# Column halves in an attention's closing step and a new state space model, in a four-layer graph network on one Trainium2 core

## The chip, the core and the metric

The kernel runs on one core of a Trainium2 chip. Its metric is the device time of one execution in microseconds (us). The kernel before takes 2626.57 us, the median of three runs that lie between 2625.1 and 2631.52 us.

The engines appear in the profile as PE (TensorE, matrix multiplication), PEld (its weight loads), DVE (VectorE), ACT (ScalarE), POOL (GpSimd) and SP (SyncE). [...]

## What is computed

The input is a matrix `x` of 2708 nodes by 256 features and a 0/1 adjacency matrix. Four layers follow one another, each a graph layer and a feed-forward layer, with a normalisation ahead of each and an addition to `x` behind it:

- layer 0: cosine attention over the graph, then the slice layer
- layer 1: graph attention with four heads, then a top-1 choice of eight experts
- layer 2: graph attention with biases, then a decoder layer (attention with a triangular mask, then the top two of eight experts)
- layer 3: graph attention with elu, then a linear layer

Two of the feed-forward layers are touched. The slice layer, with 8 heads of 64 features and 64 slices per head, is

```python
sw = softmax((xm @ W_slice.T + b_slice) / temp, axis=-1)      # [head, node, slice]
st = einsum('bhnc,bhng->bhgc', fx, sw) / (sw.sum(2) + 1e-05)  # slice tokens: 64 x 512
ot = _hydra(st, ...)                                         # state space model over 64 tokens
out = einsum('bhgc,bhng->bhnc', ot, sw); out @ out_w.T + out_b
```

and its state space model, which runs over the 64 tokens `u` in both directions, is

```python
z, xBC, dt = split(u @ in_w.T)                 # 512, 640 (x 512, B 64, C 64), 2 x 8 columns
dt = softplus(dt + dt_bias)                    # one set of 8 for each direction
xBC = silu(causal convolution of xBC, 3 taps, + conv_b)
h = h * exp(-dt * exp(A_log)) + dt * B * x     # per head and token; y = h . C
y = shift(y_forward) + shift(y_backward) + x * (x @ fcD_w.T + Dp)
yg = y * silu(z)
yg = yg * rsqrt(mean(yg**2) + 1e-05) * norm_w
return yg @ out_w.T
```

The decoder's attention has four query heads and two heads of keys and values, of 64 features each. Its output goes through `wo`, is added to the normalised input, and is routed to the experts.

## The kernel before

All activations stay on the chip in `X`, 22 tiles of 128 nodes (the last has 20). Buffers come from pools. The program's scheduler settles the order in which each engine issues its instructions, by data, buffers and priorities, except where a block fixes the order of an engine to that of the code (`manual_schedule`).

**Slice layer (`slice_ffn`, L392 to L478).** First it issues the loads of weights on POOL's queue: `outw`, `outb`, `wfx`, `bfx`, `hyin` (2336 KB) and `hyout` (1024 KB). Then `ln_stats` takes mean and variance of every tile on DVE. The loop over tiles is a pipeline of three steps: `logits` (normalise on DVE, transpose and multiply on PE), `softmax` (five operations of 128x512 and a small reciprocal on DVE, an exponential on ACT) and `products` (four transposes `pt` and four matmuls into the accumulators `z` on PE). After the last tile, L468 divides the four accumulators by their norms and gives `zs`, the slice tokens weighted with the features.

**State space model (`hydra`, L481 to L672).** It runs alone between the tile loop and the output: `zs` is transposed (L504), multiplied by `wfx` for each head (L512), copied to `u`, transposed again to `ut`. From `ut` come the gate `z` (eight matmuls of 512 columns in all), `dt`, and the convolution inputs (L539). The recurrence is unrolled: the sums of decays between each pair of tokens are made by matmuls of the 64x64 triangular matrices with the decays (L615 to L619), an exponential turns them into kernels `k`, one for each direction, and the two kernels are merged into `km` (64 x 8 x 64) on DVE. Then `py = km x` on PE (L650), the gate, the norm on DVE and ACT, another transposition `yt`, the output product with `hyout` (32 matmul instructions, each with 64 columns), and eight products with `outw` that are copied into `mix`. The constants (`dtb`, `alog`, conv taps, triangular masks, `fcd`, `dp`, `normw`) are loaded or made inside this function. Its PSUM pool has three buffers. Every engine's order is the scheduler's. After it, a loop over 22 tiles multiplies `swt` by `mix` and adds to `X` (L478).

**Decoder attention (L1860 to L2135).** The nodes are cut into column chunks `cols` of 512 queries, numbered n = 0 to 4, and a last one, 5, of 148. Each chunk has two pairs of heads (p = 0, 1); the last chunk takes both pairs together. PE's order is written by hand; the others are the scheduler's. Five kinds of work are woven together, as generators that are advanced one step at a time:

- `scores(n, p, j)` and `values(n, p, j)`: scores of key tile j against the queries of chunk n (L1974), exponential on ACT, sums on DVE (L2005), and values on PE (L1999). They go in groups of two; the values of a group follow the scores of the next.
- `close(n, p)` (L2007 to L2016): when the last key tile is through, matmuls with ones give the sums of exponentials `pd`, DVE takes the reciprocal (L2015) and multiplies by the accumulated output `po` (L2016), which gives `yt`.
- `send(n)`: `yt` times `wo` (`wy`, L139), addition to the normalised input (`xa`, L2031), addition into `X` on POOL (L2032), router logits, choice and ranking of experts (`rank`, L1630), and the rows scattered to memory in expert order by indirect DMAs on POOL (`hs`, L1651). The generator `sends` (L2088) starts `send(n)` as soon as both pairs of chunk n are closed, and advances it one step in each group.
- `project(n)`: transposes, values, and the rotated keys and queries of chunk n (`tp`, `pv`, `pj` with L1945 and L1948). The generator `projects` runs it one chunk ahead; each group advances it so far as the share of the chunk's groups that are through demands, and to its end before the chunk's first scores.

The auxiliary PSUM buffers (`aux`, two of them) are shared by `pd`, `wy`, `tp`, `pv`, `pj` and the router.

Of the kernel before, what the change touches and what calls it, by code (L numbers as in the profile page):

```python
# [392 lines left out]
def slice_ffn(net, wf, bf, early):  # L393
# [3 lines left out]
    with ExitStack() as ctx:  # L397
# [5 lines left out]
        with ExitStack() as c2:  # L403
            wp = c2.enter_context(tc.tile_pool(name="s_w", bufs=1))
            zs = wp.tile([P, 4, D + 1], F32, name="zs")
            wfx = net.load_weight(wp, a["w_fxT"], "wfx")
            bfx = wp.tile([1, HC], F32, name="bfx")
            nc.gpsimd.dma_start(bfx, a["b_fx"].partition_broadcast(1))
            hyin = net.load_weight(wp, a["hy_inT"], "hyin")
            hyout = net.load_weight(wp, a["hy_outT"], "hyout")  # L410
# [60 lines left out]
            hydra(net, wp, zs, wfx, bfx, hyin, hyout, outw, mix)  # L471
# [9 lines left out]
def hydra(net, wp, zs, wfx, bfx, hyin, hyout, outw, mix):  # L481


    nc, tc, a = net.nc, net.tc, net.a
    H, L, HC = 8, 64, 512
    ident = net.ident
    with tc.tile_pool(name="h_w", bufs=1) as w, tc.tile_pool(name="h_p", bufs=3, space=PSUM) as psum:

        def transposes(src, n, name):

            ps = psum.tile([P, n, L], F32, name="hp", tag="hp")
            for m in range(n):
                nc.tensor.transpose(ps[:, m, :], src[:, m * P : (m + 1) * P], ident[:L, :L])
            t = w.tile([P, n, L], F32, name=name)
            nc.scalar.copy(t, ps)
            return t


        zt = w.tile([P, 2, HC], F32, name="zt")
        ztr = w.tile([1, HC], F32, name="ztr")  # L500
        for c in range(2):
            ps = psum.tile([P, HC], F32, name="hp", tag="hp")
            for m in range(4):
                nc.tensor.transpose(ps[:, m * P : (m + 1) * P], zs[:, m, c * P : (c + 1) * P], ident)  # L504
            nc.scalar.copy(zt[:, c, :], ps)
        ps = psum.tile([1, HC], F32, name="hp", tag="hp")
        for m in range(4):
            nc.tensor.transpose(ps[:, m * P : (m + 1) * P], zs[:, m, D : D + 1], ident)
        nc.scalar.copy(ztr, ps)
        ps = psum.tile([L, HC], F32, name="hp", tag="hp")  # L510
        for h in range(H):
            hs = slice(h * L, (h + 1) * L)  # L512
            net.matmul_k(ps[:, hs], zt[:, :, hs], wfx[:, :, hs], last=False)
            nc.tensor.matmul(ps[:, hs], ztr[:, hs], bfx[:, hs], start=False, stop=True)
        u = w.tile([L, HC], F32, name="u")
        nc.scalar.copy(u, ps)
        ut = transposes(u, 4, "ut")


        pz = psum.tile([L, HC], F32, name="hp", tag="hp")  # L520
        net.matmul_k(pz, ut, hyin[:, :, 0:HC])
        zg = w.tile([L, HC], F32, name="zg")
        nc.scalar.activation(zg, pz, AF.Silu)
        pdt = psum.tile([L, 2, H], F32, name="hp", tag="hp")
        net.matmul_k(pdt.rearrange("p a h -> p (a h)"), ut, hyin[:, :, 1152:1168])
        dt = w.tile([L, 2, H], F32, name="dt")
        dtb = net.load_rows(w, a["dt_bias"], H, "dtb", L)
        nc.vector.tensor_tensor(dt, pdt, dtb.unsqueeze(1).to_broadcast([L, 2, H]), ALU.add)

        def conv(n, parts, offset, name):  # L530

            cw = w.tile([parts, n, 3], F32, name=f"cw{name}")
            nc.gpsimd.dma_start(
                cw, a["conv_w"][offset : offset + n * parts].rearrange("(n p) k -> p n k", p=parts)
            )
            cb = w.tile([parts, n], F32, name=f"cb{name}")
            nc.gpsimd.dma_start(cb, a["conv_b"][offset : offset + n * parts].rearrange("(n p) -> p n", p=parts))
            ps = psum.tile([parts, n, L], F32, name="hp", tag="hp")
            for m in range(n):  # L539
                o = HC + offset + m * parts  # L540
                net.matmul_k(ps[:, m, :], hyin[:, :, o : o + parts], ut)
            pad = w.tile([parts, n, L + 2], F32, name=f"pad{name}")
            nc.vector.memset(pad, 0.0)
            nc.scalar.copy(pad[:, :, 2:], ps)
            y = w.tile([parts, n, L], F32, name=f"y{name}")
            for m in range(n):
                nc.vector.tensor_scalar(
                    y[:, m, :], pad[:, m, 0:L], cw[:, m, 0:1], cb[:, m : m + 1], ALU.mult, ALU.add
                )
                for k in (1, 2):  # L550
                    nc.vector.scalar_tensor_tensor(
                        y[:, m, :], pad[:, m, k : k + L], cw[:, m, k : k + 1], y[:, m, :], ALU.mult, ALU.add
                    )
            nc.scalar.activation(y, y, AF.Silu)
            return y

        xt = conv(4, P, 0, "x")
        bc = conv(2, L, HC, "bc")
        ps = psum.tile([L, HC], F32, name="hp", tag="hp")
        for m in range(4):  # L560
            nc.tensor.transpose(ps[:, m * P : (m + 1) * P], xt[:, m, :], ident)
# [1285 lines left out]
def attention(net, route, ln2, router, weights, mixture):  # L1847
# [11 lines left out]
    with ExitStack() as ctx:  # L1859
# [228 lines left out]
        def sends():  # L2088
            for n in range(len(cols) - 1):
                while n not in closed:  # L2090
                    yield
# [419 lines left out]
```

## Time and profile before

One execution was profiled. It took 2629.6 us itself; the span of its instructions is 2627.7 us.

| | before |
|---|---|
| median of three runs | 2626.57 us |
| profiled execution, time and span | 2629.6 us, 2627.7 us |
| mean granted clock of TensorE | 0.962 |
| busy PE, DVE, ACT, POOL | 2440.1, 1479.9, 1057.7, 335.0 us |
| slice layer, load issues to first `pt` on PE | 388.08 to 410.54 us |
| state space model, last `zs` to first output matmul | 505.43 to 565.24 us |
| attention | 1535 to 1926 us |

Positions are in us from the start of the span. A line such as `PE wy L139 <- DVE yt L2016: 11.6, 4, 3.4` says that PE stood before work of tile `wy`, line 139, until DVE's work of line 2016 on tile `yt` had ended: 11.6 us in all, four times, 3.4 us the longest. In a line in order of time the columns are start, duration, engine, line, operation, output and inputs, and in square brackets how long the engine stood before it and what ended that. "x6" is a group of six like instructions. PE's clock is granted by a throttle: 1.00 is full speed, 0.50 half. Busy time of PE can include time at half clock.

### The profile page before, as it was taken

The numbers are of one execution on the slowest core, as the hardware profiler recorded it, in microseconds if no ns is written. First come the engines' busy times: TensorE is split into PE (matmuls) and PEld (weight loads), VectorE is DVE, ScalarE is ACT, GpSimd is POOL, SyncE is SP. The second block draws the span as 40 slices with busy tenths as digits, with TensorE's granted clock in tenths as the row PEclk, the third lists the DMA queues.
The fourth block names the chain that finished last, engine by engine and source line by source line (L and its number), as shares of the span: only waits on it lengthen the run. The fifth ranks groups of instructions, "written<-read, shape, count | busy, mean of one in ns | idle before, by whom it ended". The sixth has DMA issues, their size and how long they took to land. (4 is left out here: it accounts for less than half of the span.)

```text
span 2627.7 us, 32580 instructions
## 1 busy us (share of the span) xinstructions
PE 2440.1 (93%) x11674; PEld 1583.9 (60%) x11674; DVE 1479.9 (56%) x3272; ACT 1057.7 (40%) x1703; POOL 335.0 (13%) x471
## 2 busy tenths in 40 slices
PE   5899999979999998979799989999899999969998
PEld 4666765665333334568588854444367777747887
DVE  7754438546888875333554457776752222264556
ACT  3444443224887762311444423334322222234454
POOL 1000002200000000144130011221231111110002
PEclk9999999879999999989899999999989999989999
DMA  8799511000000003664310010000231111050001
GB/s 289 279 295 319 188 66 52 3 6 1 1 1 1 1 3 106 168 192 129 103 48 1 1 39 9 23 15 15 102 133 47 33 33 33 22 204 7 0 1 43
DMA packets 106874, 197.70 MB, mean 75 GB/s; under 512 B 8846, under 2 KB 63736, under 8 KB 103876
## 3 DMA queue, kind: packets, MB, share of 16 engines
q1 hardware_dynamic: 88010, 146.82, 17.8%
q0 software_dynamic: 14896, 43.89, 5.2%
q10 hardware_dynamic: 3806, 4.85, 0.6%
q8 instruction: 98, 1.61, 0.3%
q14 instruction: 64, 0.52, 0.1%
HBM read 135.82 MB, written 59.71 MB: 74 GB/s over the span
## 5 line engine op out<-in xcount | busy, mean ns | idle before, releaser
L701 DVE SCALAR_TENSOR_TENSOR e<-e,mask 128x768 f32<-128x768 f32 (+3 forms) x352 | 417.5, 1217 | 241.2 <-ACT e L700 239.2
L700 ACT ACTIVATE e<-big_p,minus_one,ratio 128x768 f32<-128x768 f32 (+3 forms) x352 | 418.6, 1226 | 280.5 <-PE acc L1432 193.1
L1432 PE MATMUL acc<-V,e 128*128 128x257 f32 x1848 | 401.9, 380 | 5.7 <-DVE e L701 5.6
L1432 PEld LDWEIGHTS acc<-V,e 128*128 128x128 f32 x1848 | 350.9, 190 | 56.9 <-issue 7.0
L2186 PE MATMUL h<-w,ft 128*128 (+1 forms) x752 | 234.6, 454 | 1.0 <-DMA f<-hs 1.0
L307 PE MATMUL acc<-F,e 128*128 128x257 f32 (+1 forms) x924 | 212.6, 383 | 4.0 <-DVE e L303 3.6
L897 PE MATMUL acc<-e,V 128*64 128x512 f32 (+1 forms) x1056 | 208.1, 547 | 1.3 <-DVE e L701 1.3
L307 PEld LDWEIGHTS acc<-F,e 128*128 128x128 f32 (+1 forms) x924 | 171.9, 190 | 56.6 <-DVE e L303 29.5
L2203 DVE TENSOR_TENSOR hh<-hh,h 128x682 f32<-128x682 f32 x47 | 40.7, 866 | 243.7 <-PE h L2186 243.7
L2186 PEld LDWEIGHTS h<-w,ft 128*128 128x128 f32 x752 | 136.1, 191 | 56.7 <-issue 1.8
L897 PEld LDWEIGHTS acc<-e,V 128*64 128x64 f32 x1056 | 73.5, 137 | 150.4 <-issue 145.0
L1983 ACT ACTIVATE e<-sc 128x1024 f32<-128x1024 f32 (+4 forms) x131 | 107.1, 863 | 136.7 <-PE sc L1974 116.6
L303 DVE TENSOR_TENSOR e<-e,mask 128x512 f32<-128x512 f32 (+2 forms) x132 | 80.4, 621 | 141.2 <-ACT e L296 139.5
L2005 DVE TENSOR_TENSOR sum<-sum,e 128x1024 f32<-128x1024 f32 (+4 forms) x131 | 134.8, 1029 | 38.3 <-ACT e L1983 23.7
L296 ACT ACTIVATE e<-score 128x512 f32<-128x512 f32 (+2 forms) x132 | 69.4, 544 | 170.8 <-PE score L294 145.4
L2218 PE MATMUL po<-w,ht 114*128 (+1 forms) x564 | 129.8, 380 | 0.9 <-DVE ht L2211 0.9
L1974 PE MATMUL sc<-qt,kt 64*128 64x512 f32 (+5 forms) x568 | 123.9, 555 | 0.9 <-ACT sum L1983 0.9
L2218 PEld LDWEIGHTS po<-w,ht 114*128 114x128 f32 x564 | 106.6, 190 | 22.4 <-DVE ht L2211 8.1
L908 PE MATMUL den<-e,low 128*3 128x512 f32 (+1 forms) x1056 | 117.7, 542 | 0.0
L294 PE MATMUL score<-QK 128*128 128x512 f32 (+2 forms) x264 | 112.2, 554 | 3.4 <-ACT e L296 3.0
L1999 PE MATMUL po<-e,V 128*64 128x512 f32 (+5 forms) x524 | 111.2, 543 | 0.3 <-DVE e L1989 0.3
L2212 ACT COPY ht<-pt 114x256 f32<-114x256 f32 x47 | 17.5, 372 | 200.7 <-DVE ht L2211 200.7
(654 smaller groups left out, 3420.2 us busy)
## 6 DMA issues: line engine op xcount, KB each, us to landing
row<-in_adj SPq DMA_DIRECT2D x21, 1354.0 KB
raw<-in_adjT SPq DMA_DIRECT2D x35, 768.0 KB
hs<-zero SPq DMA_DIRECT2D x8, 2838.0 KB
hidden<-hr SPq DMA_DIRECT2D x32, 256.0 KB
wd<-in_f_wd SPq DMA_DIRECT2D x8, 1024.0 KB
kept<-mask SPq DMA_DIRECT2D x21, 338.5 KB
mask<-kept SPq DMA_DIRECT2D x21, 338.5 KB
w<-in_d_w1T SPq DMA_DIRECT2D x8, 682.0 KB
```

The costliest lines, as they stand in the source:

```text
L294: nc.tensor.matmul(ps[:r, :iw], QK[:, 0, span(j)], QK[:, 1, i0 : i0 + iw], start=True, stop=True)
L307: ended = nc.tensor.matmul(acc[k], e[:r, k * P : (k + 1) * P], F[:r, j, :], start=j == 0, stop=j == NT - 1)
L700: nc.scalar.activation(v, big_p[:, i], AF.Relu, bias=net.minus_one, scale=ratio)
L701: return nc.vector.scalar_tensor_tensor(v, v, 1.0, net.mask[:, j, i], ALU.add, ALU.mult)
L897: nc.tensor.matmul(acc[n][half, :iw], V[:, j, h, :], e[n][:, k, :iw], start=j == 0, stop=j == NT - 1)
L908: nc.tensor.matmul(den[g : g + Q, :iw], low[:, j, h, Q - 1 - q : 2 * Q - 1 - q], e[n][:, k, :iw], start=False, stop=j == NT - 1 and q == Q ...
L1432: nc.tensor.matmul(acc[k][:ri], e[:, k * P : k * P + ri], V[:, j, :], start=j == 0, stop=j == NT - 1)
L1974: nc.tensor.matmul(by_pairs(ps[:r, g], m, iw)[:, :, o:], kt[b, span(j)], qt[b, :, o:iw], start=True, stop=True)
L1999: nc.tensor.matmul(by_pairs(outs[n, p][b], m, iw)[:, :, o:], V[:r, j, g, :], by_pairs(e[:r, g], m, iw)[:, :, o:], start=j == 0, stop=j == ...
L2005: nc.vector.tensor_tensor(total, total, by_heads(e[:r], m, iw)[:, :, :, o:], ALU.add)
L2186: last = nc.tensor.matmul(halves[s, n][:, q, :HALF], fts[s][:, c, :], weights.w13[n][:, es[s], c, q * HALF : (q + 1) * HALF], start=c == 0 ...
L2218: last = nc.tensor.matmul(po, ht[:KP, k, :], w2[:KP, es[s], k, :], start=k == 0, stop=k == KC - 1)
```

## The change

It has three parts. The line numbers of the profile are those of the kernel before.

1. **The closing step.** For the ten closes with one head pair, reciprocal and product are each issued for columns 0 to 255 and for 256 to 511. The last close is left whole.
2. **PE's order in the attention.** `sends` lets two more steps pass between the second close of a chunk and the start of `send`. A counter `quiet` is set to 2 at each close, and while it is positive no step of `projects` is taken, except in the first chunk and where a chunk's projection has to be finished for its scores.
3. **The state space model.** The function `hydra` becomes a class. Its constructor is called where the loads stood, ahead of `ln_stats`. It loads and prepares all constants there: `hyout` is multiplied by `norm_w` row by row (four DVE operations of 128x512), `exp(A_log)` is taken on ACT, triangular masks and zeroed buffers are made on POOL. `run` has a hand-written order on PE, ACT and DVE and seven PSUM buffers. The two directions lie in the two halves of the partitions, so that one DVE or ACT instruction does both; the heads write `ut` directly in transposed form, and everything behind it (gate, `y`, output) stays transposed, so that `u` and `y` are no longer transposed on PE. The gate's product comes late and has 64 columns instead of 512. The norm's sum of squares is a matmul with ones, and its factor is applied at the last eviction, four instructions of 128x256 in turn on ACT and DVE.

The diff, cut to its core:

```diff
-            wfx = net.load_weight(wp, a["w_fxT"], "wfx")
...
-            hyout = net.load_weight(wp, a["hy_outT"], "hyout")
+            layer = Hydra(net, wp)
             ln = net.ln_stats()
...
-            hydra(net, wp, zs, wfx, bfx, hyin, hyout, outw, mix)
+            layer.run(zs, outw, mix)
...
+class Hydra:
+    def __init__(self, net, pool):
...
+        self.wfx = net.load_weight(pool, a["w_fxT"], "wfx")
+        self.bfx = pool.tile([1, HC], F32, name="bfx")
+        nc.gpsimd.dma_start(self.bfx, a["b_fx"].partition_broadcast(1))
+        self.hyin = net.load_weight(pool, a["hy_inT"], "hyin")
+        self.hyout = net.load_weight(pool, a["hy_outT"], "hyout")
+        self.fcd = net.load_weight(pool, a["fcdT"], "fcd")
+        self.dtb = net.load_rows(pool, a["dt_bias"], H, "dtb")
+        self.alog = net.load_rows(pool, a["a_log"], H, "alog")
+        nc.scalar.activation(self.alog, self.alog, AF.Exp)
+        self.dp = pool.tile([H, 1], F32, name="dp")
+        nc.gpsimd.dma_start(self.dp, a["hy_d"].rearrange("(p n) -> p n", n=1))
+        normw = pool.tile([P, 4], F32, name="normw")
+        nc.gpsimd.dma_start(normw, a["norm_w"].rearrange("(c p) -> p c", p=P))
+        for c in range(4):
+            nc.vector.tensor_scalar(self.hyout[:, c, :], self.hyout[:, c, :], normw[:, c : c + 1], None, ALU.mult)
+        for name, n, parts, offset in (("bc", 2, L, HC), ("x", 4, P, 0)):
...
+            nc.gpsimd.memset(pad, 0.0)
...
+        make_upper_triangular(nc, self.seen[low])
+        make_lower_triangular(nc, self.seen[high])
+        make_upper_triangular(nc, self.rise[low])
+        make_upper_triangular(nc, self.rise[high], val=-1.0, diag=False)
+        nc.vector.tensor_scalar(self.fall, self.rise, -1.0, None, ALU.mult)
+        self.pick = pool.tile([H, H, L], F32, name="pick")
+        nc.vector.tensor_copy(self.pick, net.ident[:H, :H].unsqueeze(2).to_broadcast([H, H, L]))
+        self.km = pool.tile([P, H, L], F32, name="km")
+        nc.gpsimd.memset(self.km, 0.0)
+    def run(self, zs, outw, mix):
...
+            ps = bank([P, 4, L])
+            for h in range(H):
+                here = ps[halves[h % 2], h // 2, :]
+                nc.tensor.matmul(here, self.bfx[:, hs], ztr[:, hs], start=True, stop=False, skip_group_check=True)
+                for c in range(2):
+                    nc.tensor.matmul(
+                        here, self.wfx[:, c, hs], zt[:, c, hs], start=False, stop=c == 1, skip_group_check=True
+                    )
...
+            for b in halves:
+                nc.tensor.matmul(
+                    pk[b], self.fall[b], la[b].unsqueeze(2).to_broadcast([L, H, L]),
+                    start=True, stop=False, skip_group_check=True,
+                )
+            for h in range(H):
+                for b in halves:
+                    nc.tensor.matmul(
+                        pk[b, h, :], la[b, h : h + 1].to_broadcast([L, L]), self.rise[b],
+                        start=False, stop=True, skip_group_check=True,
+                    )
...
+            pz = bank([P, 4, L])
+            for m in range(4):
+                net.matmul_k(pz[:, m, :], hyin[:, :, m * P : (m + 1) * P], ut)
...
+            for m in range(4):
+                net.matmul_k(po[:, m, :], self.hyout[:, :, m * P : (m + 1) * P], y)
...
+            for m in range(4):
+                pm = bank([P, D])
+                for b in halves:
+                    nc.tensor.matmul(pm[b], ot[b, m, :], outw[b, m, :], start=True, stop=True, skip_group_check=True)
+                if m % 2:
+                    nc.scalar.activation(mix[:, m, :], pm, AF.Copy, scale=rs)
                 else:
+                    nc.vector.tensor_scalar(mix[:, m, :], pm, rs, None, ALU.mult)
...
-            y = results[n][:, p : p + m, :iw]
-            nc.vector.reciprocal(y, by_pairs(pd, m, iw))
-            nc.vector.tensor_tensor(y, y, by_pairs(outs.pop((n, p)), m, iw), ALU.mult)
+            po = outs.pop((n, p))
+            half = 2 * P if m == 1 else iw
+            for i in range(0, iw, half):
+                y = results[n][:, p : p + m, i : i + half]
+                nc.vector.reciprocal(y, by_pairs(pd, m, iw)[:, :, i : i + half])
+                nc.vector.tensor_tensor(y, y, by_pairs(po, m, iw)[:, :, i : i + half], ALU.mult)
...
                 while n not in closed:
                     yield
+                for _ in range(2):
+                    yield
                 yield from send(n, rp, aux)
...
+                quiet -= 1
                 for n, p in ending:
                     close(n, p)
+                    quiet = 2
...
                 while group and at[2] * len(queries[at[0]]) * (tiles_of(*cols[at[0]])[-1] + 1) < at[1] * 18:
+                    if quiet > 0 and at[0]:
+                        break
                     at[2] += 1
                     next(heads, None)
```

## The prediction

> **What bounds the kernel now.** I read the page's busy shares and clock row first, then the waits of TensorE inside the attention stage, the order in time around one of them, the costliest tile there, and tables by stretch for the state space model. The page's totals and its clock row (40 slices of 65.7 us, tenths of full speed):
>
> ```profile
> PE 2440.1 (93%) x11674; PEld 1583.9 (60%) x11674; DVE 1479.9 (56%) x3272; ACT 1057.7 (40%) x1703; POOL 335.0 (13%) x471
> PEclk9999999879999999989899999999989999989999
> ```
>
> TensorE is the bound: 188 us without work in 2628, little more than that to win. The change touches three stretches: the head of the slice stage (388 to 417 us), the model (503 to 566) and the attention (1535 to 1926). The waits of PE from 1522 to 1950 (total us, times, longest):
>
> ```profile
> engine line waited for: us in total, times, longest us
> PE wy L139 <- DVE yt L2016: 11.6, 4, 3.4
> PE pj L1945 <- DVE yt L2015: 5.9, 2, 3.6
> PE pj L1945 <- DVE xa L2031: 5.4, 1, 5.4
> ...
> PE rank L1630 <- DVE dtaken L1621: 1.7, 1, 1.7
> ```
>
> Seven of these waits end at a close: `wy` needs the product yt, and `pj` stands behind the reciprocal. One in order of time:
>
> ```profile
> 1789.46 3.35 DVE L2015 RECIPROCAL yt<-pd 128x512 f32<-128x512 f32 x1
> 1793.81 0.68 DVE L2016 TENSOR_TENSOR yt<-yt,po 128x512 f32<-128x512 f32 x1
> 1794.54 2.93 PE L139 MATMUL wy<-wo,yt 128*128 128x256 f32 x6 [3.40 <-DVE yt L2016]
> ```
>
> DVE holds yt for 5 us, PE stands 3.40 us, and the six matmuls then last 2.93 us. The same six take 1.49 us elsewhere in the stage: a half clock follows the wait.
>
> The model is another regime. Columns: stretch, length, busy us of PE, PEld, DVE, ACT and POOL, then granted clock, DMA share, GB/s:
>
> ```profile
> 503.00:508.00 5.00, 4.61 (x19) 2.95 (x19) 3.27 (x13) 1.26 (x3) 1.88 (x3) 0.53 0.04 5
> 508.00:513.00 5.00, 5.00 (x30) 3.78 (x31) 0.38 (x2) 0.27 (x1) 4.58 (x13) 0.50 0.16 6
> ...
> 518.00:523.00 5.00, 5.00 (x16) 1.67 (x15) 0.00 (x0) 1.26 (x2) 0.00 (x0) 0.76 0.00 0
> 523.00:528.00 5.00, 4.92 (x51) 4.68 (x49) 1.21 (x7) 2.25 (x5) 0.00 (x0) 1.00 0.01 3
> ...
> 533.00:538.00 5.00, 5.00 (x48) 5.00 (x48) 1.25 (x4) 2.11 (x3) 0.00 (x0) 0.50 0.00 0
> ...
> 553.00:558.00 5.00, 5.00 (x26) 5.00 (x25) 0.00 (x0) 0.00 (x0) 0.00 (x0) 0.50 0.02 3
> ```
>
> The clock is half nearly throughout, though PE counts as busy. Full clock came only in pz, eight 512-column matmuls, and lasted through the convolution. Streams of 64 columns stayed at .50 for 7 us (hyout, 552.6 to 559.7).
>
> **What the Trainium skill says.** The Trainium skill, "TensorE: Matmul & The Clock Gate", Part 1 (The HAM clock gate): half clock is the default, full clock comes after about 3.4 us of sustained activity and is lost after an idle window. The traces agree on the factor of two after a wait, and show that "busy" is not enough: 64-column streams longer than 3.4 us do not warm. "TensorEngine Tiling (Array Packing)", Key Properties: tiles run independently, and changing the mode drains the array. Here L897's 1056 matmuls of 547 ns add up to 208 us busy, so two column halves overlap; what row-and-column halves do, no row shows. "ScalarE: Activation LUTs", What ACT_TABLE_LOAD costs: about 1283 ns; the trace shows 1283.
>
> **Part 1, the closes.** Rows by tile, ten of each:
>
> ```profile
> L2015 DVE RECIPROCAL yt<-pd x10: 3342/3350/3353, 1569.8 to 1884.0; 128x512 f32<-128x512 f32 x10
> L2016 DVE TENSOR_TENSOR yt<-yt,po x10: 666/675/687, 1573.3 to 1887.9; 128x512 f32<-128x512 f32 x10
> ```
>
> In the built program DVE's order at every two-half close is reciprocal, reciprocal, product, product, with nothing between. A 128x8 reciprocal takes 0.20 us, so about 0.15 is fixed: halves are 2 x 1.75 = 3.5 against 3.35, and products 2 x 0.42 (the 128x256 xa addition) against 0.675. Each close is 0.3 us longer, 3 us of DVE in ten; DVE is busy 20 to 34 of every 40 us there, so this shows only where PE still waits, perhaps 1 us in all. Halving alone gains nothing: bounds 0 to +3 us.
>
> What can gain is PE's new order. Counted in PE entries from the last ones-matmul ahead of it, the first `wy` of chunks 0, 2, 3 and 4 (the four waits) stood 10, 10, 6 and 6 behind, and stands 42, 80, 26 and 14 behind after; that of chunk 1 goes from 32 to 6, directly behind the next chunk's first close. `pj` no longer follows a close within two groups. The 5.45 us wait for xa is another thing: chunk 1's addition into X queued on POOL behind eight indirect DMAs of chunk 0, some 10 us; rank and the next wy are 36 PE entries apart after, 10 before. So that collision should go.
>
> At stake: waits 11.6 + 5.9 + 5.4, and 1.1 of a pv wait behind the same xa, 24.0 us. The half clock after each, from the same matmuls at both speeds: wy 1.4, 0.9, 1.4, 1.0; pj and po about 6.0 together; 10.7. In all 34.7 us. What returns: wy of n = 1 at its close, about 2; n = 4, about 1; rank of n = 4 is eight PE entries nearer the end, and from rank to the landing of f 17.1 us pass (1909.2 to 1926.2), so its tail costs 2.5 to 4, say 3; projections now forced in a lump before a chunk needs them, 2 to 4, say 3; the longer closes 0.5; half clock after these, about 3. Sum 12.5. Gain 22 us, bounds 12 (everything returned doubles) to 32.
>
> **Part 2, the head of the slice stage.** Preparation moves from the model to ahead of it. On POOL it issues fcd, dtb, alog, dp, normw behind hyout, then outw, outb, four conv loads, two pads, six mask instructions and km. Issue takes 0.53 to 0.78 us each by the before's rows, affine selects 0.25, memsets 0.17 to 0.7. outw is still issued at 404.43, where it waits for DVE's last X; after it outb 0.55, cwbc and cbbc 0.6 each, cwx 0.78, cbx 0.75, and about 2.5 of masks and memsets: POOL is through at about 411.
>
> On DVE, four scalings of hyout wait for hyout (landed 403.2) and for normw, which queues behind it: 405 to 406 by its 2.8 us landing. DVE then stands at `fall`, which needs POOL's last mask, until 411.1. Behind it wait the whole softmax of the first tile and so PE's first pt. Before, DVE began that softmax at 403.71 and pt ran at 410.54; the same 6.4 us chain now starts at 411.1, with 0.2 less overlap: pt at about 417. Loss 6.5 us. From there to 502 PE is busy 38.8 of 40 us, so at most 2 come back. Bounds +4.5 to +8.5. POOL's early work saves nothing later: in the model its constants were hidden under the head matmuls (PE 5.00 of 5.00 in 508 to 513).
>
> **Part 3, the model.** Stepwise, against 565.24, the first output matmul. First transposes wait for all four zs (505.43) instead of overlapping them: +1.3. One ut directly in transposed form drops u's copy, four transposes and a second copy, -1.4; heads keep their 1.02 us each. So pdt starts at 517.75 as before. pz leaves the front, -5.3, but so does what warmed the clock: bc and x convolution cost 9.6 cold (0.222 each, the hyout rate) against 4.9 + small; end of convolution about 529.4 against 527.9. Silu of x at 533.3 against 531.1. Decay matmuls in stacked halves start at 529.4, not 532.9, and DVE forms km for both directions at once: km at 537.4 against 545.1, -7.7. Then pz returns as 16 matmul pairs of 64 columns, 7.1 cold, py 2, the gate chain about 3, po 7.1, sum of squares, ot, and mix with four 128x256 evictions against eight, -1.5; no yt transposes, -1.4. All cold I arrive at 562.9: gain 2.3. With the clock full from the decay matmuls on, the same list gives 551.7: gain 13.5. I take cold: the new streams are 64 columns wide with a few of 128 and 512, shorter than 3.4 us, the kind that stayed at .50 above. Bounds: loss 2 to gain 14.
>
> **Sum.** -22 + 6.5 - 2.3 = -17.8, and a small weight of a partly warm model: -19. The profiled execution (2629.6, span 2627.7, the rest lies around the span) becomes 2610.6; it stood 3.0 above the median, which becomes 2607.5. I say 2607. A measurement of this kernel tells about 0.3%, 8 us, from no change.
>
> **Rivals.** *Warm model* (0.18): row-and-column halves keep the array dense enough. For it: half-array tiles overlap at L897. Against: 51 instructions in 5 us did not warm at 553. -22 + 6.5 - 13.5 = -29: 2597.5.
>
> *The stalls move* (0.18): lumped projections, the second wy tile lacking its bank, and the 17 us tail take back nearly all. For it: two auxiliary banks for pd, wy and transposes. Against: DVE has a third of its time free. Attention -9, the rest +4: 2621.
>
> *Dear head* (0.09): small loads land late, pt at 425. +14 instead of +6.5: 2615.
>
> *Slower* (0.05): one mechanism, DVE at the head of the slice stage held by a load or a mask. Each us is one us of PE, for the stage has no slack. It decides from about 24 us on, plus the 8 measurable: pt later than 442. For it: normw is gathered in 4-byte pieces through a queue holding 3.3 MB. Against: that queue's longest landing is 13.1 us. At 40 us of delay: 2640.
>
> That the halves do nothing by themselves is in the order already; were PE's order harmless too, +4 + 2 would leave 2632; I count that with the stalls and the slower case.
>
> **How the numbers follow.** Likeliest case 0.50 with its own range 2598 to 2615. Faster by over 0.3% (below 2618.7): 0.50 + 0.18 + 0.08 + a fifth of the moved stalls, 0.80; same 0.14; slower 0.06. The 8-in-10 range takes in the warm model and most of the moved stalls: 2594 to 2621.
>
> **What would show it.** In the new profile: the four waits of wy on yt down to two short ones; no pj behind a reciprocal; no 5 us wait for xa; a longer wait of h for f at the end. First pt near 417 with DVE's idle ended by POOL. In the model km 7 us earlier, but pz and po at 0.222 us each and clock .50; first output matmul 4 us later than before by the clock. I am wrong if pt comes at 411, if the model's clock is 1.00, or if new waits of sc on qt appear.

## The result and the profile after

The changed kernel takes 2599.82 us, the median of four executions (2594.48 to 2609.12), against 2629.05 us for the kernel before on the same chip. The ratio is 0.9894, with a 95% interval of 0.986 to 0.9927: 28 us less, between 19 and 37. The forecast was 2607 with a range of 2594 to 2621. The time lies inside, 7 us below the likeliest case, and the way it came about differs from that case in three places.

The profiled execution of after took 2609.1 us (span 2607.2) and is the slowest of its four. So its gain on the profiled execution of before, 20.5 us, is smaller than that of the medians. The interval of after is wide because its four executions span 14.6 us; what spreads them is not shown.

The page of after, busy totals and the clock row:

```profile
PE 2422.9 (93%) x11708; PEld 1574.6 (60%) x11708; DVE 1477.6 (57%) x3288; ACT 1051.7 (40%) x1692; POOL 336.2 (13%) x476
PEclk9999999979999999989899999999989999979999
```

TensorE is still the bound at 93%. Where the time went is seen by cutting both executions at the same instructions. The stages are: *slice*, from DVE's last X of the graph layer to the first transposition of zs; *head*, the first part of it, to the first pt; *model*, from there to the first output matmul; *middle*, untouched code, to the attention's first score; *attention*, to the end of PE's last matmul there (`so_many`); *tail*, to the first expert matmul (`h`); *rest*, to the end.

| us | before | after | difference | forecast |
|---|---|---|---|---|
| slice (of it head) | 100.9 (7.2) | 111.9 (17.7) | +11.0 (+10.4) | +6.5 |
| model | 61.1 | 46.5 | -14.6 | -2.3 |
| middle | 978.9 | 978.3 | -0.6 | 0 |
| attention | 381.2 | 352.5 | -28.8 | -25, its tail left out |
| tail | 2.3 | 15.2 | +12.9 | +3 |
| rest | 700.0 | 701.1 | +1.0 | 0 |

With the start (DVE's last X 1.5 us earlier) that is the -20.5 us of the two spans. The first transposition starts before the last zs in before and behind it in after. Counted to and from the last zs, as the forecast counts, the slice stage is 9.5 us longer and the model 13.1 us shorter.

**Attention.** The waits of PE from 1522 to 1950 us (total, times, longest):

```profile
engine line waited for: us in total, times, longest us
PE tp L132 <- DMA f<-hs: 14.1, 1, 14.1
PE tp L1949 <- DVE iry L348: 5.8, 1, 5.8
PE wy L139 <- DVE yt L2049: 3.2, 1, 3.2
PE rank L1661 <- DVE dtaken L1652: 2.2, 1, 2.2
PE pj L1976 <- DVE drank L1664: 2.0, 1, 2.0
```

The four waits of wy, 11.6 us, are gone. One of 3.2 us is new, before chunk 1's wy, which now stands directly behind the next chunk's close and goes on when that close's reciprocal is through. The waits of pj behind a reciprocal (5.9) and for xa (5.4) are gone. In their place stands one wait that before had at 0.9: the first expert tile's transposition for its rows `f`, read from the scattered `hs`. The attention as a whole, before and after (stretch, length, busy us of PE, PEld, DVE, ACT, POOL, then granted clock, DMA share, GB/s):

```profile
1544.20:1925.40 381.20, 353.38 (x1630) 155.53 (x1630) 273.31 (x558) 141.76 (x210) 85.85 (x80) 0.95 0.10 34
1538.50:1890.90 352.40, 339.53 (x1631) 150.49 (x1630) 272.90 (x578) 140.44 (x208) 81.77 (x75) 0.99 0.10 36
```

About half of the 28.8 us is idle time of PE (27.8 before, 12.9 after). The other half is PE's busy time, 13.9 us less for the same work, with the clock at 0.99 instead of 0.95. The rows by tile of the closing step:

```profile
L2049 DVE RECIPROCAL yt<-pd x20: 1689/1720/1752, 1564.1 to 1855.9; 128x256 f32<-128x256 f32 x20
L2050 DVE TENSOR_TENSOR yt<-yt,po x20: 355/380/408, 1567.4 to 1857.8; 128x256 f32<-128x256 f32 x20
```

A half costs 1.72 and 0.38 us, against 3.35 and 0.675 for the whole. Two halves added up would be 0.2 us dearer, but issued together they overlap: the pair takes 3.36 and 0.68 us (shown with e3 below).

**Tail.** Behind the attention, first before (POOL's scatter and reads, SP's load of the next weights), then after. The columns are start, duration, engine, line, operation:

```profile
1911.76 0.99 POOL L1651 DMA_INDIRECT hs<-h,dto  x1 [15.47 <-DVE h L1649]
1924.50 2.76 POOL L1773 DMA_DIRECT2D f<-hs  x5 [0.33 <-issue]
1925.12 2.85 SPq L1521 DMA_DIRECT2D w<-in_d_w3T  x5
```

```profile
1880.96 0.99 POOL L1682 DMA_INDIRECT hs<-h,dto  x1 [14.61 <-DVE h L1680]
1898.39 2.75 POOL L1804 DMA_DIRECT2D f<-hs  x5 [0.39 <-issue]
1890.66 16.85 SPq L1552 DMA_DIRECT2D w<-in_d_w3T  x8
```

Before, POOL's reads of f were issued 12.7 us after the first scatter, and the loads of w3 (eight of 682 KB) 0.6 us later, behind them. In after the attention ends earlier against its scatter, the loads of w3 go out 9.7 us after the first scatter, and POOL's reads of f follow 7.7 us behind the loads.

**Model.** The table by stretch (length, busy us of PE, PEld, DVE, ACT, POOL, then granted clock, DMA share, GB/s):

```profile
533.00:538.00 5.00, 5.00 (x26) 3.65 (x27) 1.62 (x8) 1.96 (x3) 0.00 (x0) 0.50 0.00 0
538.00:543.00 5.00, 4.88 (x73) 4.57 (x69) 3.35 (x10) 3.99 (x5) 0.00 (x0) 0.93 0.00 0
543.00:548.00 5.00, 3.53 (x45) 3.11 (x43) 1.99 (x5) 0.58 (x3) 0.00 (x0) 1.00 0.00 0
548.00:553.00 5.00, 5.00 (x28) 5.00 (x28) 0.00 (x0) 1.60 (x2) 0.00 (x0) 0.59 0.01 3
```

The clock rises during the decay matmuls and stays up through px, pz and py. It falls again at about 549, behind the pauses around py (PE busy 3.53 of 5 us from 543 to 548), and most of the product with hyout runs cold. That the pauses are the cause is not shown.

**Head.** DVE at the start of the slice stage, after:

```profile
401.78 0.47 DVE L327 SCALAR_TENSOR_TENSOR X<-F,s,X 20x256 f32<-20x256 f32 x1
402.63 0.38 DVE L124 TENSOR_SCALAR f<-X,mv,rstd 128x256 f32<-128x256 f32 x1
...
411.47 0.25 DVE L519 TENSOR_SCALAR fall<-rise 128x64 f32<-128x64 f32 x1 [6.42 <-POOL rise masks.py:66]
...
411.90 0.68 DVE L433 TENSOR_TENSOR sw<-pl,bf 128x512 f32<-128x512 f32 x1
```

The stand at `fall` is there, 6.42 us, ended by POOL's last mask, as forecast. But something else is there too: the normalisation `f` of tile 0 comes at 402.63. Before had it at 388.12, and so had the tile's logits ready when X was:

```profile
388.12 0.41 DVE L124 TENSOR_SCALAR f<-X,mv,rstd 128x256 f32<-128x256 f32 x1
...
403.71 0.68 DVE L437 TENSOR_TENSOR sw<-pl,bf 128x512 f32<-128x512 f32 x1
```

A part is clock as well: the last four matmuls of pl ahead of the first pt take 3.68 us in after (from 415.69) and 1.99 us in before (from 408.15).

### The profile page after: what moved, and what is told of

Read it like the earlier page. It is cut to its first block, busy times and chain, and to the rows that moved or that the text cites. A ratio compares the mean times of both kernels' runs of the same rounds, so it can differ in the third digit from the quotient of the medians.

```text
span 2607.2 us, 32662 instructions
## 1 busy us (share of the span) xinstructions
PE 2422.9 (93%) x11708; PEld 1574.6 (60%) x11708; DVE 1477.6 (57%) x3288; ACT 1051.7 (40%) x1692; POOL 336.2 (13%) x476
```

## The experiments

Each ratio is to the kernel before on the same chip, with its 95% interval. It is not the quotient of the two medians (e2 has 0.9903, its medians 0.9915); gains over before are taken from the ratios. The experiments ran in three groups on three chips: the median of before was 2628.34 us beside e1 to e4, 2631.03 beside e5 to e8 and 2628.58 beside e9 to e12. Where stage lengths are given they are those of the profiled execution, cut as in the table above.

### The two halves of the change apart

`e1_model_only` joins the new model with the old attention, `e2_attention_only` the old model with the new attention. `e3_halves_only` is before with the loop over the two halves alone (the lines with `half` in the diff above), and `e4_order_only` is e2 with this edit undone, so that only `sends` and `quiet` are new.

> The new state space model with the attention of before. Read from the two traces: first pt of the slice stage 10.5 us later against the stage's own start, model 14 us shorter from last zs to first output matmul, sum -3: 3 us below before, within 0.3% of it. Rival, all of the gain comes from the model: 20 us or more below before. The forecast on record (model cold, gain 2.3, head loss 6.5) gives 4 us above before.

> The model of before with the attention of after (halves and order). Theory: the attention's PE work ends about 29 us earlier counted from its own start, and 12 to 13 us of it are given back in one wait for f from hs behind it: 16 us below before, with that wait at 12 to 15 us in the trace. Rival, the wait at the end is an accident of the one profiled execution: 26 us below before and a wait under 5 us.

> Before with the reciprocals and products in column halves and nothing else. Theory of the forecast: DVE runs reciprocal, reciprocal, product, product, each close 0.3 us longer, so 0 to 3 us above before and the four waits of wy on yt stay at 11 to 14 us. Rival, the halves let PE start wy on the first half: those waits shrink by half or more and the time falls by 5 us or more.

> Before with PE's new order (two steps of delay, quiet groups) and whole reciprocals. Theory: the same as attention only, 16 us below before, within 3 us of that run. Rival, the order pays only with the halves: 8 us or less below before.

| | median us | ratio to before | slice | model | attention | tail |
|---|---|---|---|---|---|---|
| before | 2628.34 | | 100.9 | 61.1 | 381.2 | 2.3 |
| e1 model only | 2625.11 | 0.9992 (0.9982 to 1.0002) | 109.1 | 46.2 | 383.3 | 2.3 |
| e2 attention only | 2605.95 | 0.9903 (0.9888 to 0.9918) | 101.2 | 62.4 | 359.2 | 2.1 |
| e3 halves only | 2621.88 | 0.9969 (0.9958 to 0.9981) | 100.5 | 60.7 | 375.9 | 2.1 |
| e4 order only | 2611.14 | 0.9927 (0.9913 to 0.9941) | 100.5 | 62.1 | 348.3 | 16.3 |

The parts add: 0.08% and 0.97% make 1.05%, and the whole change gives 1.06%. **The new model gives no gain that is clear of noise**: 2 us, between 5 less and 1 more, where 3 were expected. What it wins inside, 15 us, the late slice stage takes back for more than half (+8.2 in e1, +11.0 in after). The gain of the change is the attention's.

**The halves alone gain 8 us** (5 to 11), where 0 to 3 us of loss was expected. One reason is in the order of DVE at a close. Before, the scheduler had put a sum between the reciprocal and the product (in time, before):

```profile
1789.46 3.35 DVE L2015 RECIPROCAL yt<-pd 128x512 f32<-128x512 f32 x1
1792.73 1.16 DVE L2005 TENSOR_TENSOR sum<-sum,e 128x1024 f32<-128x1024 f32 x1
1793.81 0.68 DVE L2016 TENSOR_TENSOR yt<-yt,po 128x512 f32<-128x512 f32 x1
1794.54 2.93 PE L139 MATMUL wy<-wo,yt 128*128 128x256 f32 x6 [3.40 <-DVE yt L2016]
```

The same close in e3:

```profile
1783.79 3.36 DVE L2018 RECIPROCAL yt<-pd 128x256 f32<-128x256 f32 x2
1787.06 0.68 DVE L2019 TENSOR_TENSOR yt<-yt,po 128x256 f32<-128x256 f32 x2
1787.48 2.53 PE L139 MATMUL wy<-wo,yt 128*128 128x256 f32 x6 [2.02 <-DVE yt L2019]
```

From the reciprocal's start to wy it is 5.1 us before and 3.7 in e3. The sum no longer comes between (1.1 us), and wy starts when the first of the two products is through. The order of DVE is the same at all ten closes: before, one other DVE instruction stands between reciprocal and product each time, and the close takes 4.1 to 5.0 us from the reciprocal's start to the product's end; in e3 none stands there, and it takes 3.96 to 3.97 us. The waits of wy on yt fall from 11.6 us to this, still four:

```profile
PE wy L139 <- DVE yt L2019: 7.3, 4, 2.2
```

and the attention is 5.4 us shorter. The rival had asked for half of the waits; 4.3 of 11.6 us went. Of the 7.7 us between the two profiled executions 2.3 lie in stages that the edit does not touch, so the gain of the halves may lie at the lower end of its interval. A part of what I had called the price of the reciprocal was the place of another instruction.

**The order alone** shortens PE's attention by 32.9 us, nearly as much as the 34.7 that stood at stake, and then loses 14 at the tail:

```profile
PE tp L132 <- DMA f<-hs: 15.1, 1, 15.1
```

In e2 that wait is missing, in code that has the same order:

```profile
PE pd L2013 <- DVE sum L2005: 4.0, 1, 4.0
...
PE tp L132 <- DMA f<-hs: 0.5, 1, 0.5
```

DVE stood 3.22 us in this execution just before the attention's last sum, for nothing that the profile shows. The loads of w3 wait for that sum, so they came behind the reads of f, and nothing collided. So the rival expectation, that the long wait belongs to some executions only, is half right: of the seven profiled executions whose order at the tail is that of after (after, e2, e4, e5, e8, e10, e11), six have it, at 12.3 to 15.2 us, and one has not. By the ratios e4 is 19 us below before and e2 25.5; 16 was expected of both. Whether the halves add anything on top of the order stays open: the medians say 5 us (2611.14 and 2605.95, intervals that touch), the two attention stages say the opposite.

### The tail: who is ahead of whom

`e6_tail` takes the delay away for the last chunk that is sent inside the attention, so that its scatter starts earlier:

```diff
-                for _ in range(2):
+                for _ in range(2 if n + 2 < len(cols) else 0):
                     yield
```

`e9_held` leaves the order of PE as in after and puts the loads of w3 behind the first read of f on SP's queue (that read was ACT's):

```diff
         core.close()
-        weights.more()
         mixture(exp, lambda *work: send(len(cols) - 1, *work))
...
-                fetch(s, (nc.scalar if s < 3 else nc.gpsimd) if cut else None)
+                fetch(s, (nc.scalar if 0 < s < 4 else nc.gpsimd if s else None) if cut else None)
+                if cut and s == s0:
+                    held = route.loaded
+            if cut:
+                with tc.issue_after(held.ins):
+                    weights.more()
```

> After, with no delay of two steps for chunk 4 alone (the last that is sent inside the attention). Theory: rank and the scatter to hs come some 4 us earlier before the attention's end, so that scatter and reads of f are nearly through before the loads of w3 start; the wait for f falls from 14.1 to 2 to 8 us, while a wait of wy on yt of about 2 us and its half clock return: 4 to 9 us below after. Rival, the loads of w3 start whenever the attention ends and delay f in any case: wait still above 11 us, time within 2 us of after.

> After, with the loads of w3 queued on SP behind the first read of f (that read moves from ACT to SP). Theory: the 14.1 us wait for f is the loads of w3 getting ahead of the scatter and the reads; held back, the wait is what the scatter needs by itself, 12.3 us from its first issue (the traces without the collision) plus 2.2 for the read, so 3 to 6 us of PE wait, and the time is 8 to 11 us below after in its bad order, about 2592. Rival, the late w3 is then waited for by h: a new wait of h on w3 of 5 us or more and no gain.

In e6 the median is 2600.76 us, ratio 0.9881 (0.9866 to 0.9896). Scatter and loads still cross, by less: first scatter 1880.92, w3 at 1892.64, reads of f at about 1894. The wait is 7.4 us instead of 14.1, inside the expected 2 to 8, and the wait of wy at the last close is back at 2.2. The median does not lie 4 to 9 us below that of after (2599.82), which was not measured beside it. Beside e6 ran e8, described below, whose head, model and attention with tail are within 0.5 us of after's: 2608.5 us, ratio 0.9919 (0.9906 to 0.9933). Against it e6 is 7.7 us less, and the intervals are apart.

In e9 the median is 2601.66 us, ratio 0.9895 (0.9879 to 0.9911). SP, and the wait of PE:

```profile
1900.28 0.35 SPq L1804 DMA_DIRECT2D f<-hs  x1
1901.33 8.43 SPq L1552 DMA_DIRECT2D w<-in_d_w3T  x8
```

```profile
1903.16 0.66 PE L132 MATMUL tp<-ident,f 128*128 128x128 f32 x2 [6.03 <-DMA f<-hs]
```

Attention and tail together are 359.7 us against 367.7 in after: 8.0 us less, as expected, and h does not wait for w3. With the loads held, f is there 16.0 us after the first scatter (1887.15 to 1903.16); in after it took 24.0 (1880.96 to 1904.96), in before 14.5. That the loads of w3 delay the scatter and the reads by 8 us is thereby shown. The other profiles agree: from the first scatter to f 22.2 to 24.0 us pass where the loads go out first (after, e4, e5, e8, e10, e11) and 14.4 to 17.3 where they come behind the reads (before, e1, e2, e3, e7, e9, e12). The rest of the wait is there because scatter and reads need 14 to 16 us by themselves, while the attention goes on for 9.9 us after the first scatter (13.6 before).

The 8 us do not show in the median of e9 against that of after (2601.66 and 2599.82). They do between e11 and e12 below, which ran side by side and differ only in the held loads: 2603.59 and 2594.94 us, with attention and tail 368.7 and 360.2 us. The two intervals of the ratios still touch. Whether some executions of after escape the collision is open. The spread of the times is no sign of it: e1, without the long wait, spreads over 19.7 us in 21 executions, the longer the lower their granted clock (0.967 at 2617.53 us, 0.957 at 2637.19).

### The head: one stand behind another

`e5_head` makes the masks and the zeroed km ahead of all loads on POOL and issues `outw` and `outb` behind the model's loads:

```diff
-        outw = net.load_weight(big, a["out_wT"], "outw")
+        outw = big.tile([P, HC // P, D], F32, name="outw")
...
             layer = Hydra(net, wp)
+            nc.gpsimd.dma_start(outw, a["out_wT"].rearrange("(c p) m -> p c m", p=P))
...
         self.net, self.pool = net, pool
+        self.rise, self.fall, self.seen = (pool.tile([P, L], F32, name=n) for n in ("rise", "fall", "seen"))
...
         self.wfx = net.load_weight(pool, a["w_fxT"], "wfx")
```

`e7_head_tail` is e5 and e6 together. `e10_place` is after with all small buffers of the constructor (taps, masks, km and the rest) in a pool at the other end of the memory, so that f lies where it lay before:

```diff
-            layer = Hydra(net, wp)
+            layer = Hydra(net, wp, c2.enter_context(tc.tile_pool(name="s_x", bufs=1, side="right")))
...
-            early.close()
             layer.run(zs, outw, mix)
```

`e11_head_place` is e5 with that placing, `e12_all` is e11 with the held loads of e9.

> After, with the masks and the zeroed buffer made ahead of the loads on POOL, and outw and outb issued behind the model's loads; nothing else. Theory: DVE's stand of 6.4 us at fall is what makes the head late; without it first pt comes 7 to 10 us earlier against the stage's start and the time falls by 8 to 10 us against after. Rival, the scaling of hyout or the table load on ACT sets the start: first pt at most 2 us earlier, time unchanged.

> Both edits, masks first and no delay for chunk 4. The two lie 1400 us apart, so the gains should add: 12 to 19 us below after, near 2584 where after stands at 2600. Less than 8 would say that one of them is taken back later.

> After, with the small prepared buffers in a pool at the other end of the memory, so that the buffers of f lie where they lay before; POOL's order stays. Theory: half of the head's loss is not POOL but f of tile 0, which lies in after where PE's last product of the layer before still reads (first f of the stage at 402.6 where before had it at 388.1); with it back, two tiles' softmax runs before DVE comes to fall: first pt 6 to 9 us earlier against the stage's start, time 6 to 9 us below after. Rival, POOL's mask holds DVE as before: first pt at most 3 us earlier.

> Masks first and the small buffers at the other end: both causes of the late head taken away. Theory: the interval from DVE's last X of the layer before to the first pt returns from 17.7 us to the 7.2 us of before, within 1 us; time 9 to 11 us below after. Rival, the scaling of hyout (1.6 to 2.2 us on DVE, waits for its load) still stands ahead: 10 us or more in that interval.

> Both causes of the head's loss taken away and w3 held behind f: the gains lie apart and add, 17 to 21 us below after, about 2581, and faster than every kernel so far. Less than 10 would say that what is won at the head is lost again before the attention's end.

| | median us | ratio to before | head | slice | attention + tail |
|---|---|---|---|---|---|
| before | | | 7.2 | 100.9 | 383.6 |
| after | 2599.82 | 0.9894 (0.986 to 0.9927) | 17.7 | 111.9 | 367.7 |
| e5 masks first | 2604.62 | 0.9908 (0.9893 to 0.9923) | 13.5 | 107.8 | 367.5 |
| e7 and no delay | 2597.65 | 0.9871 (0.9855 to 0.9886) | 14.4 | 108.7 | 357.8 |
| e10 other place | 2607.13 | 0.9927 (0.9915 to 0.9939) | 12.9 | 110.2 | 365.6 |
| e11 both | 2603.59 | 0.9913 (0.9899 to 0.9927) | 12.2 | 107.3 | 368.7 |
| e12 and w3 held | 2594.94 | 0.9885 (0.9868 to 0.9902) | 12.2 | 107.3 | 360.2 |

None of the edits of the head brings back 7.2 us, and the expectations of e5, e10 and e11 failed in size. The reason is a chain of stands, of which each edit removes one and uncovers the next. In e5, DVE passes `fall` early and then meets the scaling of hyout:

```profile
391.64 0.20 DVE L493 TENSOR_SCALAR fall<-rise 128x64 f32<-128x64 f32 x1 [1.02 <-POOL rise masks.py:66]
...
407.01 2.24 DVE L512 TENSOR_SCALAR hyout<-hyout,normw 128x512 f32<-128x512 f32 x4 [0.89 <-DMA normw<-in_norm_w]
```

while f of tile 0 is as late as in after (405.12). The place in memory is what makes it late, as e10 shows; that the work it has to wait for there is the graph layer's last product (L91) is read from the built program and no profile shows it. In e10 and e11 f is back at its old place in time, and the first softmax addition runs at 403.7 as before. But the place at the other end comes free only with the last X, so in e11 POOL starts the masks at 403.9 and all small loads behind them:

```profile
406.46 0.20 DVE L492 TENSOR_SCALAR fall<-rise 128x64 f32<-128x64 f32 x1 [1.45 <-POOL rise masks.py:66]
...
411.37 1.99 DVE L511 TENSOR_SCALAR hyout<-hyout,normw 128x512 f32<-128x512 f32 x4 [1.34 <-DMA normw<-in_norm_w]
```

The rival of e11, that the scaling of hyout stands ahead, is what happened. So the head's loss has at least three parts that cover each other: the masks on POOL, the place of f, the scaling that waits for normw. No run takes the scaling away, so its part is read from the order in time only. Which is worth how much alone cannot be read from these runs; together, what the edits got back is 4 to 5.5 of 10.4 us.

Against after none of these medians is separated: after has four executions, not measured beside these, and all the intervals overlap with its own. By that comparison e7 and e12 gain 2 and 5 us, where 12 to 21 was expected, and e5, e10 and e11, with waits at the tail of 12.8, 13.5 and 12.3 us, gain nothing. Compared with what ran beside them they come closer to the expectations. Against e8, e5 is 3.9 us less (the intervals overlap), e6 7.7 and e7 10.9 (the intervals are apart), so the parts add, while e7 was expected at 12 to 19. Against e11, e12 is 8.7 us less. Both e7 and e12 are faster than before, by 1.0 to 1.5% with their intervals.

### The clock in the model

`e8_narrow` replaces the two wide decay matmuls by pairs of 64 columns, with the same sums:

```diff
-            for b in halves:
-                nc.tensor.matmul(
-                    pk[b], self.fall[b], la[b].unsqueeze(2).to_broadcast([L, H, L]),
-                    start=True, stop=False, skip_group_check=True,
-                )
             for h in range(H):
+                for b in halves:
+                    nc.tensor.matmul(
+                        pk[b, h, :], self.fall[b], la[b, h : h + 1].to_broadcast([L, L]),
+                        start=True, stop=False, skip_group_check=True,
+                    )
                 for b in halves:
```

> After, with the two decay matmuls of 512 columns (four instructions with the two halves) replaced by sixteen pairs of 64 columns that compute the same. Theory: [...]without them the clock in the model stays at .50 past 545 us, pz and the rest double, and the first output matmul comes 5 to 8 us later. Rival, concurrent halves of 64 columns are dense enough by themselves: clock full by 541 us again, time within 2 us of after.

The median is 2608.5 us, ratio 0.9919 (0.9906 to 0.9933), with a long tail wait of 15.2 us in the profile. The model takes 46.2 us, after 46.5. In the model the rival is right: nothing wide is needed. Its forecast of the time, within 2 us of after, missed by the medians (2599.82), though the intervals of the ratios overlap and head, slice stage and attention with tail are as long as after's within 0.5 us. In time, the decay matmuls of one head in e8, and of before:

```profile
538.87 0.42 PE L617 MATMUL hp<-la,fall 64*64 64x64 f32 x4
539.09 0.42 PE L622 MATMUL hp<-rise,la 64*64 64x64 f32 x4
```

```profile
534.69 0.42 PE L615 MATMUL hp<-upper,la 64*64 64x64 f32 x2
534.90 0.42 PE L616 MATMUL hp<-la,nupper 64*64 64x64 f32 x2
```

A step of 0.21 us carries four instructions in e8 and two in before, since the two partition halves run beside each other. Both streams fill PE's busy time completely. Before's ran 6.7 us at a clock of .50 throughout (532.9 to 539.6); that of e8 has the full clock after 3.1 us (537.1 to about 540.2):

```profile
538.00:540.00 2.00, 2.00 (x44) 2.00 (x42) 2.00 (x11) 1.20 (x2) 0.00 (x0) 0.50 0.00 0
540.00:542.00 2.00, 2.00 (x39) 1.72 (x35) 0.99 (x3) 1.77 (x3) 0.00 (x0) 0.95 0.00 0
```

What has to be dense is not the multiplications. The stream with hyout in before does as many and stayed at .50:

```profile
552.60 7.09 PE L139 MATMUL hp<-yt,hyout 128*128 128x64 f32 x32 [0.46 <-ACT yt L495]
```

Estimated from these lines, both do 4.7 to 5.0 million multiplications per us, 32 times 128x128x64 in 7.09 us here and four times 64x64x64 in 0.21 us in e8. What differs is the data that streams in, rows times columns: about 37,000 elements per us for hyout and 39,000 for the decays of before, neither of which woke the clock, and 78,000 in e8. The pz of before, three matmuls of 128x512 at 0.87 us each ahead of the rise, comes to 75,000, and its clock rose after 2.7 us (517.75 to about 520.4). The streamed data fit these four streams; a threshold was not measured.

## Why the prediction was right, and where not

**The closes: right in the order, wrong on the halves.** Of the waits named, wy of n = 1 came as forecast (3.2 us; I had about 2), wy of n = 0, 2, 3 went, n = 4 had no wait (I had 1), pj behind a reciprocal and the collision on xa are gone, no wait of sc on qt came. The sum of 34.7 us at stake was sound, its split less so: e4 won 32.9, 17.7 in idle time of PE (24.0 of waits were counted) and 15.2 in its busy time (10.7 of half clock). The step that failed is "Halving alone gains nothing". It took each close as 0.3 us longer by adding the fixed part of two reciprocals; back to back the pair takes 3.36 us against 3.35. And it compared the new order of DVE with nothing: the old order had a sum of 1.16 us between reciprocal and product. The lines shown in the prediction have the gap, from 1792.81 to 1793.81 us, without asking what filled it. Measured: 8 us of gain (5 to 11).

**The tail: right mechanism, size wrong.** I wrote that rank of n = 4 is eight entries nearer the end and that its tail costs 2.5 to 4, say 3. It is 3.65 us nearer (9.94 us from first scatter to the end, 13.59 before). The cost was 12.9. What I did not ask is which transfer starts when the attention ends: the loads of w3, 5.5 MB, which had gone out 0.6 us behind the reads of f before and now went ahead of them. Holding them gave 8.0 us back in the profile; the other 4.9 are near the 3 that I had.

**The head: right mechanism, size too small.** The stand at `fall` was put at 411.1 and came at 411.5, 6.42 us long. Its cost was put at 6.5, bounds 4.5 to 8.5; it was 10.4 in after (7.5 to 10.4 in the runs with the same start), of which the place of f and a cold clock ahead of the first pt are parts. Of the 10.4 us 0.9 came back by the last zs, where at most 2 was forecast. That a larger pool moves the buffers behind it, and so the work that a first write has to wait for, was in no step. That the masks alone set the loss is refuted by e5.

**The model: the rival was right.** "I take cold" failed. The list for the warm case gave a gain of 13.5, and 13.1 came by the same count. The argument, 64-column streams stay at .50, left out that the new streams run as pairs of halves. The clock of 1.00, which the prediction names as a sign of being wrong, is there from about 538.7 to 549. The rival with this cause had 0.18 and the time 2597.5, 2 us from the measured median. That nearness is partly chance, since two errors cancel: it had the model with its head at -7 us, where e1 measured -2, and the attention with its tail at -22, where e2 measured -25.5.

**The sum.** Forecast -19, measured -28 by the ratio. By parts: model and head +4.2 forecast, -2 measured (e1); attention with its tail -22 forecast, -25.5 measured (e2). By the stages of the profiled executions the likeliest case was short by 10.8 us in the model and 3.8 in the attention, and too hopeful by 3.9 at the head and 9.9 at the tail. That these nearly cancel is luck; the time lies in the range because the range had room for the warm model. The slower case did not come: the late head cost 10 us, where 24 were needed to decide.

**Readings that were off.** Six of the waits listed, not seven, end at a close; the seventh is that for xa. The lower bound of 12 us, "everything returned doubles", is 9.7 by its own sum (34.7 less 25.0). The durations of L897 do not show that halves overlap, since the records of a single stream overlap too: hyout's last 0.42 us, and one begins every 0.21. L897's starts, in pairs 0.02 us apart, do show it. None of the three changes the argument.

## What to carry to other kernels

When a stage ends earlier, list the transfers that its end releases and what they will now overtake; a short read behind a long load on other queues cost 8 us here. Read the new order of an engine against the old one, not against a sum of durations: the place of one 1.2 us addition was worth more than the reciprocal's cut. Work prepared early is free only if the memory and the queues it takes are free as well; look at what the first write into each moved buffer waits for.

## What was not expected of the hardware

- The throttle does not go by busy time. A stream of 64-column matmuls on one half of the partitions at a time, busy 100% for 6.7 us, stayed at half clock; the same matmuls issued as pairs on both halves, twice as many per microsecond, had the full clock after 3.1 us. The Trainium skill, "TensorE: Matmul & The Clock Gate", Part 1, gives about 3.4 us of sustained activity; here it was 2.7 us (pz of before) and 3.1 (e8). That activity is not a busy engine is what before and e8 add; the multiplications per microsecond do not explain it either, and the streamed data do in the streams looked at above.
- Two 128x256 reciprocals issued together take 3.36 us, one of 128x512 takes 3.35: cutting costs 0.01 us.
- In the untouched middle stage (972.7 to 985.4 us over all fourteen profiled kernels), the length varies by 13 us, which bounds what a difference of a few us between two profiled executions can say. Between the two extremes, e5 and e7, 10.3 of the 12.7 us are busy time of PE (914.2 and 924.6 us); the cause is open.
